# Turned rows go through a scratch in DRAM, and the second norm's rows of blocks 1 to 13 are turned that way

## The chip, the cores and the metric

The kernel runs on one core of a Trainium2 chip. The metric is the device time of one execution in microseconds (us). The core has a TensorE for matmuls (PE), a VectorE (DVE), a ScalarE (ACT), a GpSimd (POOL) and a SyncE (SP), which work through their own instruction queues in order and wait for each other by semaphores. Tiles lie in SBUF or, for results of TensorE, in PSUM. Copies are carried by 16 DMA engines; here practically all copies are issued by SP.

## The reference

A transformer block with adaptive layer norm on `x` of 8 x 1024 x 512 in float32, 16 heads of 32, hidden size 2048:

```python
mod = jax.nn.silu(condition) @ Wada + bada
sh_a, sc_a, gt_a, sh_m, sc_m, gt_m = jnp.split(mod, 6, axis=1)
xn = _layernorm(x, g1, be1)
xm = xn * (1.0 + sc_a[:, None, :]) + sh_a[:, None, :]
x = x + gt_a[:, None, :] * _attention(xm, Wqkv, Wproj, bproj)
xn = _layernorm(x, g2, be2)
xm = xn * (1.0 + sc_m[:, None, :]) + sh_m[:, None, :]
h = jax.nn.gelu(xm @ W1 + b1, approximate=False)
x = x + gt_m[:, None, :] * (h @ W2 + b2)
```

`_attention` is causal multi-head attention with a softmax.

## The kernel before

The rows are cut into 16 blocks of 512 tokens (`blocks`, numbered n; two to a batch entry). For each block there are linear steps: k, q and v projections, the output projection `proj`, the up projection in four parts `u(n,0)` to `u(n,3)`, and the down projection in four parts. The projections use Strassen's scheme: seven products of 256 x 256 tiles in place of eight, from a modulated and transposed input `xm` and three sums and differences of its quarters, `t`. Next to them runs the attention of each block, in score units (`sc`: TensorE writes the scores, VectorE masks them and takes the maxima `mx`) and weight units (`st`: TensorE writes the scores again, ScalarE takes the exponential `pT`, TensorE multiplies with v into `po`). Score units and weight units share one tile of four PSUM banks with a single buffer (`ps_st`), so each such unit waits until the last user of that tile has been read. Three more PSUM banks (`banks`, in the profile `bank`) serve the linear steps.

The order on every engine is written out by a planner that runs when the program is built: it keeps an assumed time for each engine (`now`) and for each tile (`written`, `left`), and always emits the linear thread that would wait least, or attention units where these are behind their pace (`step_aside`, `work`). A thread gives what it needs next by `yield`. The list `plan` sets the order of the linear steps: in window w, with n = w - 1, `proj(n)` is followed by `mt(n)`, which makes the input of the up projection, then by `k` and `q` of block w + 1 and by `u(n,0)`. When the planner finds the linear threads more than 3 us away and all three banks free, it may write a score unit head by head into the banks (`scores_by_heads`).

Weights come through a ring of nine buffers (`wp`, `fetch`): SP issues the load of a piece as soon as the piece nine places earlier has been used. SP's queue is in order, so a copy that waits holds all that stand behind it.

Layer norm (`normalize`) writes normalized rows into the tile `hat` (one buffer), with the tokens in the partitions; the projections need the features there. `modulated(key, ...)` does this turning and applies gain and shift, in one of two ways:

- Keys in `by_pe`: TensorE transposes each 128 x 128 piece into a bank (line 722, 16 transposes a block), and ScalarE or VectorE reads it from there into `xm` (lines 726 and 732).
- Other keys: VectorE transposes within squares of 32 x 32 (line 664, four instructions, into `xm`), and 16 copies of 64 KB from SBUF to SBUF, back into `hat`, move the squares to their places (line 673, function `turn`). ScalarE or VectorE then reads `hat` into `xm`. The order of the tokens differs for these keys; the code in `down` undoes it where it picks columns of `hT`.

Before the change `by_pe` holds every `m` key (the second norm, blocks 0 to 15), and `a0` and `a1`; the `a` keys of blocks 2 to 15 go the second way. `GATHERING` is the time that the planner assumes from the issue of these copies to their end.

## Time and profile before

| what | value |
|---|---|
| median of 3 runs | 3577.96 us (3577.63 to 3582.41) |
| span of the profiled execution, first to last instruction | 3570.9 us |
| TensorE matmuls, mean granted clock | 98% of the span busy, 0.997 |
| VectorE, GpSimd, ScalarE | 61%, 58%, 33% busy |
| bytes moved by DMA | 447 MB, 125 GB/s on the mean |
| copies `hat_a<-xm_a` (line 673) | 224, 64 KB each |

The profiled execution has no separate time; its span stands for it, and the median of the runs is 7.1 us above that span. A row of a group gives line, engine, operation, tiles (written <- read), shapes, count, then busy time in us and the mean duration of one in ns, then the idle time ahead of the group with what ended it. float32 matmuls show as two records each. Busy times of matmuls overlap, so their sum over groups is more than the engine's busy time. A row of the waits gives who waited for whom, then the total in us, the number of waits and the longest. In the timeline the first two figures are the start and the length of a piece in us, and in brackets the idle time before it. A window row gives a stretch, its length, the busy time and count of each engine, the granted TensorE clock, the share of the DMA engines in use and GB/s.

### The profile page before, as it was taken

The numbers are of one execution on the slowest core, as the hardware profiler recorded it, in microseconds if no ns is written. First come the engines' busy times: TensorE is split into PE (matmuls) and PEld (weight loads), VectorE is DVE, ScalarE is ACT, GpSimd is POOL, SyncE is SP. The second block draws the span as 40 slices with busy tenths as digits, with TensorE's granted clock in tenths as the row PEclk, the third lists the DMA queues.
The fourth block names the chain that finished last, engine by engine and source line by source line (L and its number), as shares of the span: only waits on it lengthen the run. The fifth ranks groups of instructions, "written<-read, shape, count | busy, mean of one in ns | idle before, by whom it ended". The sixth has DMA issues, their size and how long they took to land.

```text
span 3570.9 us, 120927 instructions
## 1 busy us (share of the span) xinstructions
PE 3495.3 (98%) x54621; PEld 1749.3 (49%) x54621; DVE 2179.7 (61%) x2393; ACT 1187.1 (33%) x1232; POOL 2080.9 (58%) x2246
## 2 busy tenths in 40 slices
PE   8999899999999999999999999999999999999999
PEld 4444445445554445545454455544545445455445
DVE  5876575564755657465574656746666566565663
ACT  2334333242333513235142342423423134231421
POOL 2667746665466664667545775366762667526660
PEclk9999999999999999999999999999999999999999
DMA  6753433434434344433444334443344433434334
GB/s 200 235 174 93 128 93 110 135 105 138 115 109 131 108 141 113 135 107 105 142 118 146 99 101 141 120 140 102 102 131 124 140 105 104 126 111 140 91 113 137
DMA packets 318934, 447.12 MB, mean 125 GB/s; under 512 B 29516, under 2 KB 179852, under 8 KB 318164
## 3 DMA queue, kind: packets, MB, share of 16 engines
q1 hardware_dynamic: 318304, 439.36, 41.7%
q8 instruction: 430, 7.05, 0.8%
q14 instruction: 84, 0.69, 0.1%
q10 hardware_dynamic: 116, 0.03, 0.0%
HBM read 394.12 MB, written 28.38 MB: 118 GB/s over the span
## 4 chain that ended last, share of the span: by engine, by line
PE 88%; POOL 4%; DMA 3%; DVE 2%; SPq 2%; issue 1%; ACT 1%; ACTq 0%; DVEq 0%; POOLq 0%
PE bank L202 60%; PE sc L1511 8%; PE po L1644 7%; PE st L1604 7%; PE st L1592 2%; POOL pT L1734 2%; PE bank L1665 2%; DMA w<-in_L_cond_Wproj_dram 1%; PE bank L722 1%; SPq L673 1%; POOL hT L161 1%; DVE mx L1528 1%; DMA out_dram<-xr 0%; PE bank L1566 0%; DMA w<-in_L_cond_Wada_dram 0%
## 5 line engine op out<-in xcount | busy, mean ns | idle before, releaser
L1734 POOL TENSOR_TENSOR pT<-pT,pT 128x256 f32<-128x256 f32 (+3 forms) x1254 | 1215.4, 1005 | 335.5 <-PE po L1644 182.2
L1616 ACT ACTIVATE pT<-st 128x2048 f32<-128x2048 f32 x288 | 541.0, 1878 | 1171.6 <-PE st L1604 1074.2
L202 PE MATMUL bank<-w,hT 128*32 128x256 f32 x14336 | 813.0, 380 | 1.1 <-ACT rec L1674 0.9
L1528 DVE TENSOR_REDUCE mx<-sc 128x4 f32<-128x2048 f32 (+3 forms) x384 | 665.8, 1754 | 223.3 <-PE sc L1511 217.1
L202 PEld LDWEIGHTS bank<-w,hT 128*32 128x32 f32 x14336 | 453.0, 110 | 365.7 <-issue 81.0
L202 PE MATMUL bank<-xm_m,w 128*32 128x256 f32 x8192 | 498.2, 380 | 0.0
L202 PE MATMUL bank<-t_m,w 128*32 128x256 f32 x6144 | 383.4, 380 | 0.1
L1621 POOL TENSOR_SCALAR_AFFINE_SELECT pT<-pT 128x512 f32<-128x512 f32 x256 | 168.1, 675 | 344.6 <-ACT pT L1616 344.6
L202 PEld LDWEIGHTS bank<-xm_m,w 128*32 128x32 f32 x8192 | 257.2, 110 | 219.9 <-issue 54.6
L1511 PE MATMUL sc<-kT,qT 32*128 32x512 f32 (+3 forms) x3072 | 329.1, 520 | 2.7 <-DVE mx L1528 1.7
L1525 DVE TENSOR_TENSOR sc<-sc,mask 128x1024 f32<-128x1024 f32 (+1 forms) x160 | 162.7, 1017 | 265.5 <-PE sc L1511 177.5
L1644 PE MATMUL po<-pT,v 128*32 128x512 f32 (+3 forms) x3048 | 303.0, 492 | 2.1 <-POOL pT L1621 2.1
L1604 PE MATMUL st<-qT,kT 32*128 32x512 f32 (+3 forms) x3072 | 301.5, 488 | 0.0
L202 PEld LDWEIGHTS bank<-t_m,w 128*32 128x32 f32 x6144 | 190.2, 110 | 180.8 <-issue 58.1
L202 PE MATMUL bank<-w,qT 128*32 128x512 f32 x2048 | 240.7, 599 | 10.6 <-DMA w<-in_L_cond_Wproj_dram 10.5
L202 PE MATMUL bank<-xm_a,w 128*32 128x256 f32 x3968 | 246.0, 383 | 2.1 <-ACT p_k L188 2.0
L1683 DVE RECIPROCAL rec<-rec 128x128 f32<-128x128 f32 x256 | 224.5, 918 | 33.0 <-ACT rec L1674 33.0
L1511 PEld LDWEIGHTS sc<-kT,qT 32*128 32x128 f32 x3072 | 129.3, 183 | 173.1 <-ACT pT L1616 65.7
L202 PE MATMUL bank<-t_a,w 128*32 128x256 f32 x2944 | 189.6, 382 | 0.4 <-ACT xm_m L732 0.4
L193 DVE TENSOR_TENSOR hT<-bank,u_u 128x512 f32<-128x512 f32 x192 | 129.1, 684 | 98.2 <-PE bank L202 96.9
L1058 ACT ACTIVATE hT<-hT,cols 128x512 f32<-128x512 f32 x256 | 164.4, 711 | 54.6 <-DVE hT L193 54.0
L202 PEld LDWEIGHTS bank<-xm_a,w 128*32 128x32 f32 x3968 | 123.6, 110 | 110.8 <-issue 33.4
(216 smaller groups left out, 3405.6 us busy)
## 6 DMA issues: line engine op xcount, KB each, us to landing
w<-in_L_cond_W_dram SPq DMA_DIRECT2D x384, 256.0 KB
w<-kept_up_S SPq DMA_DIRECT2D x256, 256.0 KB
w<-kept_down_S SPq DMA_DIRECT2D x256, 256.0 KB
w<-kept_qkv_S SPq DMA_DIRECT2D x180, 256.0 KB
w<-in_L_cond_Wqkv_dram SPq DMA_DIRECT2D x147, 256.0 KB
hat_a<-in_x_dram SPq DMA_DIRECT2D x64, 256.0 KB
w<-in_L_cond_Wproj_dram SPq DMA_DIRECT2D x64, 256.0 KB
xr<-in_x_dram SPq DMA_DIRECT2D x64, 256.0 KB
```

What stands on the lines that cost most here:

```text
L193: nc.vector.tensor_tensor(out, src, other, op)
L202: nc.tensor.matmul(ps[r, :], columns, rhs, start=start, stop=stop, skip_group_check=True)
L1058: nc.scalar.activation(hT[:, i, :], hT[:, i, :], AF.Gelu, bias=cols[:, O_B1 + f : O_B1 + f + 1])
L1511: nc.tensor.matmul(sc[:, j, c0 : c0 + w], qTs[n][r, gg, ts(qt, P)], keys_of(n, kh)[r, gg, :w], start=True, stop=True, skip_group_check=True,)
L1525: nc.vector.tensor_tensor(place, place, shape_of.to_broadcast(place.shape), ALU.add)
L1528: nc.vector.tensor_reduce(maxima[n, gg][:, kh, qt, :], sc[:, :, c0 : c0 + w], axis=AX.X, op=ALU.max)
L1604: nc.tensor.matmul(st[:, j, c0 : c0 + w], kT[r, gg, ts(k % NTT, P)], qT[r, gg, TB - w :], start=False, stop=True, skip_group_check=True,)
L1616: nc.scalar.activation(pT[:, :, :used], st[:, :, :used], AF.Exp, scale=scale)
L1621: nc.gpsimd.affine_select(diagonal, diagonal, pattern=[[0, HPG], [1, P]], compare_op=ALU.is_ge, fill=0.0, base=0, channel_multiplier=-1,)
L1644: nc.tensor.matmul(po[r, TB - w :], v[:, k % NTT, g * P + j * hd : g * P + (j + 1) * hd], pT[:, j, c0 : c0 + w], start=(k == 0), stop=last ...
L1683: nc.vector.reciprocal(some, some)
L1734: nc.gpsimd.tensor_tensor(into, into, pT[:, j, c0 : c0 + w], ALU.add)
```

## The change

`by_pe` now holds `a0`, `a1`, `m0`, `m14` and `m15` only, so that the `m` keys of blocks 1 to 13 are turned by VectorE and copies as well. In `turn` the 16 copies from SBUF to SBUF are replaced by one write of the whole tile (1 MB) into a scratch in DRAM, `held`, of which there are two in turn, and four reads of 256 KB from it into `hat`. The planner is told of two waits in place of one: 8 us from the write to the reads, and 8 us from the reads to their use.

```diff
-    by_pe = {f"m{n}" for n in range(NB)} | {"a0", "a1"}
+    by_pe = {"a0", "a1", "m0", f"m{NB - 2}", f"m{NB - 1}"}
...
         for t in range(NTT):
             add_job(lambda t=t: turn_tile(t), [("hat", key, t)], key[0] == "m")
         yield [("blocks", key)], []
+        held = kept.tile([P, NTT * D], F32, tag=f"held_{turns[0] % 2}", name=f"held_{key}")
+        turns[0] += 1
+        nc.sync.dma_start(held, small_blocks)
+        written["held", key] = now["PE"] + HOLDING
+        yield [("held", key)], []
         for m in range(NTT):
-            for a in range(NTT):
-                nc.sync.dma_start(rows[ts(m, Q), a, :], small_blocks[ts(a, Q), ts(m, D)])
-        written["turned", key] = now["PE"] + GATHERING
+            some = held[:, ts(m, D)].rearrange("(a i) d -> i a d", i=Q)
+            nc.sync.dma_start(rows[ts(m, Q), :, :], some)
+        written["turned", key] = now["PE"] + HOLDING
         yield [("turned", key)], []

-    GATHERING = 16000
+    HOLDING = 8000
+    turns = [0]
```

Since the planner places every instruction by these times, the change also moves other instructions on all engines. The built program has 208 transposes fewer on TensorE, 52 square transposes more on VectorE, 135 copies for the turning in place of 224 (27 writes and 108 reads), and 24 matmuls of `scores_by_heads` that were in the ordinary score units before. Lines behind the change are numbered six higher than in the profile of before.

## The prediction

> **What bounds the kernel now.** I read the page first (busy times, then the chain of waits), then the groups of instructions by line and shape, then who waits for whom, and last the timeline and the windows around the places that these named.

> ```profile
> span 3570.9 us, 120927 instructions
> PE 3495.3 (98%) x54621; PEld 1749.3 (49%) x54621; DVE 2179.7 (61%) x2393; ACT 1187.1 (33%) x1232; POOL 2080.9 (58%) x2246
> PE 88%; POOL 4%; DMA 3%; DVE 2%; SPq 2%; issue 1%; ACT 1%; ACTq 0%; DVEq 0%; POOLq 0%
> ```

> TensorE is busy 98% of the span and carries 88% of the chain. It is idle for about 3570.9 - 3495.3 = 76 us in all. So work taken off TensorE shortens the run, and every new idle microsecond on it lengthens the run. What its idle time now consists of:

> ```profile
> PE bank L202 <- DMA w<-kept_qkv_S: 11.7, 7, 2.2
> PE bank L202 <- DMA w<-in_L_cond_Wproj_dram: 10.5, 12, 1.9
> PE bank L202 <- DMA w<-in_L_cond_Wqkv_dram: 3.7, 1, 3.7
> ...
> PE st L1592 <- DVE mx L1528: 8.5, 6, 3.2
> PE sc L1511 <- DVE mx L1528: 1.7, 1, 1.7
> PE sc L1511 <- ACT pT L1616: 1.0, 1, 1.0
> ```

> The first three are waits for weights, 25.9 us; the view cut to 600 to 3060 us gives the same three figures. The last three, 11.2 us, are waits for the one score tile in PSUM (the names `sc` and `st` share one buffer).

> **The change part by part.**

> *1. Transposes taken off TensorE: -32 us.* Blocks 1 to 13 lose 16 transposes each, 208 of the 256 in this row:

> ```profile
> L722 PE MATMUL bank<-ident,hat_m 128*128 128x128 f32 x256 | 43.4, 294 | 4.3 <-ACT hat_m L651 3.3 <-ACT hat_m L624 1.0
> ...
> 1366.30 0.55 PE L722 MATMUL bank<-ident,hat_m 128*128 128x128 f32 x3
> 1366.78 0.64 PE L202 MATMUL bank<-t_a,w 128*32 128x256 f32 x8
> 1367.35 0.77 PE L722 MATMUL bank<-ident,hat_m 128*128 128x128 f32 x5
> 1368.04 1.07 PE L202 MATMUL bank<-t_a,w 128*32 128x256 f32 x16
> 1369.05 1.09 PE L722 MATMUL bank<-ident,hat_m 128*128 128x128 f32 x8
> 1370.07 0.64 PE L202 MATMUL bank<-t_a,w 128*32 128x256 f32 x8
> ```

> By the row they cost at most 43.4 x 208/256 = 35.3 us. From start to start, one block's 16 take 0.48 + 0.69 + 1.02 = 2.19 us, 28.5 us for 13 blocks. I take -32.

> *2. The burst on SP's queue goes: -18 us.* Each of 14 `a` blocks issues 16 small copies in a row:

> ```profile
> 618.93 10.75 SPq L673 DMA_DIRECT2D hat_a<-xm_a  x16
> ...
> L389 SPq DMA_DIRECT2D hat_a<-in_x_dram x56: 315/423/1502, 54.5 to 2916.5; - x56
> ```

> For 10.75 us no weight piece behind them is issued, and the weight waits above follow these bursts. In the change one write and four reads of the second row's shape take their place. At about 0.5 + 4 x 0.42 = 2.2 us of issue, the burst is no longer there. If all of it were caused by the burst, -25.9 us. Against that, the bytes of an `a` turn double to 2 MB, and 13 `m` turns of 2 MB are new: 40 MB, 9% of the 447 MB that are moved now. The reads also hold the queue until the write has landed, with Wproj pieces behind them. So the other end is above nothing: 14 turns at 0.7 us, +10. I take -18, nearer to the end at which the queue is free.

> *3. The new hop itself: hidden, if it takes what a 1 MB move takes here.* No scratch of this size exists before; the nearest row is the one move of 1 MB:

> ```profile
> 425.90 0.53 SPq L981 DMA_DIRECT2D v<-v_early  x1
> 426.40:431.00 4.60, 4.50 (x76) 2.44 (x72) 3.08 (x3) 1.07 (x2) 0.29 (x1) 1.00 0.90 310
> ```

> It is issued at 425.9 and fills the DMA engines (share 0.90) until about 431: 5.1 us. Write and reads: some 10 us, and with other loads between them 8 to 20. What covers them stands in the built order of the changed kernel's instructions: from the last product of `proj(n)` to the first product of `u(n,0)` I add up 37 to 48 us of TensorE work in blocks 2 to 13 (19 or 37 before, mostly). Normalized rows are there early in even blocks:

> ```profile
> 1102.00 1.06 PE L202 MATMUL bank<-w,qT 128*32 128x512 f32 x8
> 1121.00 2.93 ACT L624 ACTIVATE hat_m<-xr,offset_m,rstd_m 128x512 f32<-128x512 f32 x4 [1.91 <-POOL offset_m L608]
> ```

> That is 1121.0 + 2.9 - 1103.1 = 21 us behind the projection; 4 transposes, 10 us of hop and 2 us of modulation bring it to some 36 us. So in even blocks the hop costs nothing. What would wait with it if the cover were gone: behind the modulation on ScalarE the first evacuations of `u(n,0)`, on VectorE the next score reduction, and behind the reads on SP the next pieces of W1, of which nine lie ready by then.

> *4. What fills that wait: +52 us, the term that decides.* The cover is made of k and q of the next block, and when these run out, of attention alone. Then there is nothing to put between two users of the one score tile. The order around `u(5,0)` reads, shortened to its first words:

> ```
> 4107 L202 bank<-t_a7 x15
> 4108 L1517 sc_7_0_0_0 x4
> 4110 L1517 sc_7_0_1_0 x4 [waits DVE]
> 4113 L1598 st_6_3_0 [waits DVE]
> ...
> 4126 L202 bank<-xm_m5 [waits DMA, DVE]
> ```

> Here TensorE must stand until VectorE has reduced one score unit, twice. The trace of before has one such place:

> ```profile
> 439.06 1.14 PE L1511 MATMUL sc<-kT,qT 32*128 32x512 f32 x8 [1.00 <-ACT pT L1616]
> 443.40 0.61 PE L1592 MATMUL st<-mrow,minus_ones 32*128 32x512 bf16 x4 [3.20 <-DVE mx L1528]
> ...
> 440.32 0.70 DVE L1525 TENSOR_TENSOR sc<-sc,mask 128x512 f32<-128x512 f32 x1 [2.84 <-issue]
> 441.05 2.29 DVE L1528 TENSOR_REDUCE mx<-sc 128x4 f32<-128x2048 f32 x1
> ```

> Scores end at 440.20, mask and reduction end at 443.34, and the next user starts at 443.40. I went through both orders and summed, for each pair of neighbours on that tile, how much the TensorE work between them falls short of what the other engine needs:

> ```profile
> L1528 DVE TENSOR_REDUCE mx<-sc 128x4 f32<-128x2048 f32 x192 | 439.8, 2290 | 220.0 <-PE sc L1511 217.1
> L1616 ACT ACTIVATE pT<-st 128x2048 f32<-128x2048 f32 x288 | 541.0, 1878 | 1171.6 <-PE st L1604 1074.2
> ```

> (2.29 us for a reduction of 2048 columns, less for narrower ones, a mask where there is one, 1.88 us for an exponential, 0.2 to 0.3 us of handing over.) Before: 15 us; after: 76 us, nearly all of the difference right ahead of `u(n,0)`, most at blocks 1, 3, 5 and 11. Of the 15 the waits show 11.2, a factor of 0.74. So +45 to +61; I take +52. These waits stay even where the rows are there early, since TensorE keeps its order.

> *5. Six score units go head by head through the three banks* (24 matmuls of `scores_by_heads`, none before). The fourth head waits for a bank that VectorE empties, behind a 2.29 us reduction: up to 2 us each, 0 to 12; I take +6.

> *6. VectorE gets 52 transposes more.*

> ```profile
> L664 DVE STREAM_TRANSPOSE xm_a<-hat_a 128x512 f32<-128x512 f32 x56 | 34.6, 671 | 0.0
> ```

> That is 52 x 0.671 = 35 us on an engine that is idle 39% of the time, so most is hidden. In five blocks two of them stand directly ahead of the first reduction of the stretch in (4): 5 x 1.34 = 7 us if the cover is gone. 0 to 7; I take +4.

> *7. The clock: +13 us.* After a standstill TensorE runs at half rate for a while (columns: stretch, length, busy, clock, DMA share, GB/s):

> ```profile
> 388.00:390.70 2.70, 0.03 (x4) 1.00 0.00 0
> 391.10:394.40 3.30, 3.30 (x20) 0.50 0.00 0
> ...
> 855.70:857.90 2.20, 0.02 (x3) 1.00 0.79 249
> 858.70:862.00 3.30, 3.30 (x40) 0.50 1.06 339
> 113.20:116.20 3.00, 0.02 (x2) 1.00 1.05 384
> 116.20:122.00 5.80, 5.76 (x136) 1.00 1.01 345
> 3052.30:3056.00 3.70, 0.04 (x4) 1.00 0.64 179
> 3056.90:3060.20 3.30, 3.30 (x29) 0.50 1.03 375
> ```

> Three of these four waits bring 3.3 us at 0.50, that is some 1.7 us of lost work. The list in (4) has 11 waits of 2.3 us or more, in seven blocks: 11 x 3/4 x 1.7 = 14, one or two drops of before fall away with (2), and a double wait may bring two stretches: 0 to 28; I take +13. [...]

> *Sum:* -32 - 18 + 0 + 52 + 6 + 4 + 13 = +25 us. Against the profiled execution: span 3570.9 + 25 = 3596. The median of the runs, 3577.96, lies 7.1 us above that span (what is outside first and last instruction), so I forecast 3603 us. For this kernel 0.2%, 7 us, is about what can be told from no change.

> **The rivals.**

> *The saving wins (faster).* Place: the stretch ahead of `u(n,0)`; price: all that it costs, (4) to (7), 75/13 = 5.8 us a block by my sum. It decides from (32 + 18)/13 = 3.8 us a block down. For it speaks that the count overrates (0.74 above) and that the whole 25.9 us of weight waits follow the bursts. Against it, that the waits are fixed in the order. With -35.3 - 25.9 + 45 and nothing else: -16, 3562 us.

> *They cancel (same).* A seam of about 3.8 us: 3578 us.

> *The clock stays up (slower, but less).* If the waits of 2.3 to 2.6 us leave the clock at full rate, as the one at 113.2 did, term (7) is nothing and the time 3590 us. Against it speak the three others in that fence. [...]

> *The turned rows come late (slower still).* In blocks 1, 3 and 11 the reads stand directly behind the write, and the last transposes directly behind the last q product. There the cover is some 10 us of attention and 8 us of its own waits, against 13 us of hop and modulation. For it speaks that weights in flight share the engines (share 1.06 at 858.7); against it, 310 GB/s at 426. If write and reads take 10 us each, `u(n,0)` starts 7 us late in five blocks, with as many more clock drops: 35 + 14, in all +74, 3652 us.

> **How the numbers follow.** My forecast 0.46, the clock stays up 0.10, the saving wins 0.20, they cancel 0.12, late rows 0.12. Slower: 0.46 + 0.10 + 0.12 = 0.68; same 0.12; faster 0.20. The likeliest's own range is 3585 to 3632. To leave out no more than 2 in 10 the range goes from 3562 (the faster case's own value) to 3645 (just short of the late rows').

> **What would show it.** The `L722` row falls from 256 to 48 and its busy time to some 8 us (1). The weight waits on `kept_qkv` and Wproj fall under 10 us (2). TensorE's waits for `mx` and `pT` grow from 11 to about 60 us, placed right ahead of the first products on `xm_m` (4), with a granted clock of 0.50 behind several of them (7). No TensorE wait of more than 1 us on the rows read back (3). Wrong: if the waits for `mx` stay under 30 us, or if the span falls although they grow, (2) was worth more than all weight waits together.

## The result, and the profile after

The changed kernel takes 3627.14 us (median of 4 runs, 3622.46 to 3636.23) against 3577.8 us of the kernel before on the same chip: ratio 1.0147, 95% interval 1.0135 to 1.016, some 52 us slower by the ratio (the medians differ by 49.3 us). The profiled spans differ by 3620.6 - 3570.9 = 49.7 us. The page of the changed kernel (span, busy times, chain of waits by engine):

```profile
span 3620.6 us, 120483 instructions
PE 3488.6 (96%) x54413; PEld 1735.5 (48%) x54413; DVE 2193.8 (61%) x2448; ACT 1197.2 (33%) x1251; POOL 2079.0 (57%) x2240
PE 85%; DVE 6%; DMA 4%; POOL 2%; ACT 1%; issue 1%; SPq 1%; ACTq 0%; DVEq 0%; POOLq 0%
```

TensorE is idle for 3620.6 - 3488.6 = 132 us, 56 more than before, and its busy time falls by 7 us only, although the transposes went as said (groups of instructions, row of the second norm's transposes; it was 43.4 us):

```profile
L728 PE MATMUL bank<-ident,hat_m 128*128 128x128 f32 x48 | 8.3, 310 | 3.4 <-ACT hat_m L651 3.4
```

So 35 us of work left and some 29 us of slower work took its place. The recorded clock says the same: between 100 us and the last microseconds, 0.50 is granted in six stretches before, 24 us in all, and in 16 stretches after, 82 us; half of the 58 us between them is 29 us of lost work. The idle time, from the view of who waits for whom (us in total, number of waits, longest):

```profile
PE st L1598 <- DVE mx L1534: 34.2, 26, 3.8
PE sc L1517 <- DVE mx L1534: 15.1, 9, 3.1
PE bank L1485 <- DVE mx L1504: 10.2, 6, 2.2
PE bank L202 <- ACT v L188: 9.7, 3, 5.2
PE po L1650 <- POOL pT L1627: 7.1, 2, 5.5
...
PE bank L202 <- DMA w<-in_L_cond_Wproj_dram: 6.9, 5, 2.9
...
PE sc L1517 <- ACT pT L1622: 5.9, 5, 2.6
...
PE st L1598 <- ACT pT L1622: 3.1, 4, 1.1
...
PE bank L202 <- ACT p_v L188: 2.2, 2, 1.5
...
PE bank L202 <- DVE u_v L193: 2.1, 1, 2.1
```

Waits for the score tile (the two rows of `mx` on line 1534 and the two of `pT` on line 1622) go from 11.2 to 58.3 us, and those of the scores taken head by head (line 1485) are 10.2 us where there was nothing: +57. Weight waits go from 25.9 to 6.9 us: -19. New are 14 us behind `v`, `p_v` and `u_v`, and 5 us behind GpSimd at the end. With the row of transposes and the clock: -35 + 29 + 57 - 19 + 14 + 5 = +51, against 49.7 measured.

The waits behind `v` are turned rows that come late. ScalarE and VectorE wait for the rows of the first norm that were read back (the same view, of ScalarE and of VectorE):

```profile
ACT xm_a L738 <- DMA hat_a<-held_a: 74.5, 12, 11.8
...
DVE xm_a L732 <- DMA hat_a<-held_a: 44.1, 9, 8.7
```

Before, the same two rows were 7.6 and 1.5 us. The turned rows of the second norm are waited for too, but less: 12.8 us by ScalarE and 14.6 us by VectorE, 5.7 us at the longest, and TensorE's own waits for `xm_m` are 1.8 us. One place where rows of the first norm come late, in the timeline (start, duration, engine, in brackets the idle time ahead):

```profile
1948.65 0.38 SPq L673 DMA_DIRECT2D held_a<-xm_a  x1
...
1961.18 1.31 SPq L1104 DMA_DIRECT2D out_dram<-xr  x2
...
1963.08 1.81 SPq L678 DMA_DIRECT2D hat_a<-held_a  x4
...
1971.55 2.22 ACT L738 ACTIVATE xm_a<-hat_a,shifta,gaina 128x512 f32<-128x512 f32 x3 [6.92 <-DMA hat_a<-held_a]
1973.68 0.56 ACT L188 COPY v<-bank 128x512 f32<-128x512 f32 x1
...
1974.30 3.55 PE L202 MATMUL bank<-w,t_a 128*32 128x256 f32 x32 [5.18 <-ACT v L188]
```

The four reads are issued 14 us after the write, behind an output store in SP's queue; the rows can be used 8.5 us later; an evacuation of `v` (the copy of a result out of its bank) that needs none of them stands behind the modulation in ScalarE's queue, and TensorE waits for that one. No row of TensorE's own waits names the late rows.

The last thing to see is how far the two kernels are apart along the run, by the end of the last product of `proj(n)` in each trace: after block 1 the changed kernel is 10.7 us ahead, after block 7 it is 15.4 us behind, after block 14 34.4 us, after block 15 49.2 us. So nearly 15 us of the 50 are lost in the last block, in which nothing is turned differently.

### The profile page after: what moved, and what is told of

It is laid out like the page before. It is cut to its first block, busy times and chain, and to the rows that moved or that the text cites. A ratio compares the mean times of both kernels' runs of the same rounds, so it can differ in the third digit from the quotient of the medians.

```text
span 3620.6 us, 120483 instructions
## 1 busy us (share of the span) xinstructions
PE 3488.6 (96%) x54413; PEld 1735.5 (48%) x54413; DVE 2193.8 (61%) x2448; ACT 1197.2 (33%) x1251; POOL 2079.0 (57%) x2240
## 4 chain that ended last, share of the span: by engine, by line
PE 85%; DVE 6%; DMA 4%; POOL 2%; ACT 1%; issue 1%; SPq 1%; ACTq 0%; DVEq 0%; POOLq 0%
PE bank L202 59%; PE sc L1517 8%; PE po L1650 6%; PE st L1610 6%; DVE mx L1534 3%; PE st L1598 2%; PE bank L1671 2%; DMA hat_a<-held_a 1%; POOL pT L1740 1%; DMA hat_m<-held_m 1%; DMA w<-in_L_cond_Wproj_dram 1%; DVE sc L1531 1%; ACT pT L1622 1%; SPq L678 0%; ACT xm_a L738 0%
## 5 line engine op out<-in xcount | busy, mean ns | idle before, releaser
L1622 ACT ACTIVATE pT<-st 128x2048 f32<-128x2048 f32 x288 | 541.0, 1879 | 1097.2 <-PE st L1610 987.9
L202 PE MATMUL bank<-w,hT 128*32 128x256 f32 x14336 | 818.0, 380 | 0.0
L1534 DVE TENSOR_REDUCE mx<-sc 128x4 f32<-128x2048 f32 (+3 forms) x378 | 652.1, 1746 | 217.1 <-PE sc L1517 211.2
L202 PEld LDWEIGHTS bank<-w,hT 128*32 128x32 f32 x14336 | 447.1, 110 | 381.7 <-issue 98.1
L202 PE MATMUL bank<-xm_m,w 128*32 128x256 f32 x8192 | 497.7, 384 | 1.8 <-DVE xm_m L732 1.0
L202 PE MATMUL bank<-t_m,w 128*32 128x256 f32 x6144 | 378.5, 380 | 0.9 <-DVE t_m L748 0.8
L202 PEld LDWEIGHTS bank<-xm_m,w 128*32 128x32 f32 x8192 | 256.6, 111 | 227.8 <-issue 51.9
L1517 PE MATMUL sc<-kT,qT 32*128 32x512 f32 (+3 forms) x3024 | 328.3, 521 | 21.4 <-DVE mx L1534 15.1
L202 PEld LDWEIGHTS bank<-t_m,w 128*32 128x32 f32 x6144 | 191.5, 110 | 163.5 <-issue 34.8
L1689 DVE RECIPROCAL rec<-rec 128x128 f32<-128x128 f32 x256 | 225.7, 920 | 54.5 <-ACT rec L1680 54.5
L202 PE MATMUL bank<-w,qT 128*32 128x512 f32 x2048 | 243.4, 606 | 7.0 <-DMA w<-in_L_cond_Wproj_dram 6.9
L202 PE MATMUL bank<-xm_a,w 128*32 128x256 f32 x3968 | 244.2, 382 | 0.2 <-DVE u_q L193 0.2
L1517 PEld LDWEIGHTS sc<-kT,qT 32*128 32x128 f32 x3024 | 129.7, 184 | 211.3 <-issue 86.7
L1714 POOL TENSOR_TENSOR qT<-top,rec 128x512 f32<-128x512 f32 x61 | 82.1, 1345 | 198.2 <-DVE rec L1689 177.6
L202 PE MATMUL bank<-t_a,w 128*32 128x256 f32 x2944 | 183.7, 380 | 0.0
L202 PEld LDWEIGHTS bank<-xm_a,w 128*32 128x32 f32 x3968 | 124.5, 110 | 109.0 <-issue 32.3
```

Source lines behind the costliest of these rows:

```text
L202: nc.tensor.matmul(ps[r, :], columns, rhs, start=start, stop=stop, skip_group_check=True)
L1517: nc.tensor.matmul(sc[:, j, c0 : c0 + w], qTs[n][r, gg, ts(qt, P)], keys_of(n, kh)[r, gg, :w], start=True, stop=True, skip_group_check=True,)
L1534: nc.vector.tensor_reduce(maxima[n, gg][:, kh, qt, :], sc[:, :, c0 : c0 + w], axis=AX.X, op=ALU.max)
L1622: nc.scalar.activation(pT[:, :, :used], st[:, :, :used], AF.Exp, scale=scale)
L1689: nc.vector.reciprocal(some, some)
L1714: nc.gpsimd.tensor_tensor(qTs[n][:, g, :], top, rec, ALU.mult)
```

## The experiments

The ratio after each is that to the kernel before, run on the same chip between the runs of the experiment, with its 95% interval; "us" beside a ratio is (ratio - 1) x 3575.

**The two halves of the change.** `a_scratch` keeps the second norm on TensorE, `m_scratch` keeps the 16 copies for the `a` rows.

```diff
# a_scratch, to the changed kernel
-    by_pe = {"a0", "a1", "m0", f"m{NB - 2}", f"m{NB - 1}"}
+    by_pe = {f"m{n}" for n in range(NB)} | {"a0", "a1"}
# m_scratch, in turn()
+        if key[0] == "a":
+            for m in range(NTT):
+                for a in range(NTT):
+                    nc.sync.dma_start(rows[ts(m, Q), a, :], small_blocks[ts(a, Q), ts(m, D)])
+            written["turned", key] = now["PE"] + GATHERING
+            yield [("turned", key)], []
+            return
```

> The change for the `a` rows alone: every second norm stays on TensorE as before, the 14 `a` turns go by one write and four reads. TensorE's built order is nearly that of before, so there are no new seams. Theory 1 (what the trace after suggests): the weight waits fall by about 19 us, but the turned `a` rows come late through SP's queue, and TensorE stands 5 to 15 us behind the evacuations that wait with them on ScalarE and VectorE; net -15 to 0, 3563 to 3578 us. Rival (term 2 of the forecast in full, nothing comes late): -18 or better, 3550 to 3561 us, and no TensorE wait on v's evacuations.

> The change for the `m` rows alone: blocks 1 to 13 through the scratch, the `a` rows by their 16 copies as before. Theory 1 (seams and the clock are the loss): transposes -32, waits for the score tile +57, clock +25, weight waits stay at some 25 us: +45 to +65, 3623 to 3643 us. Rival (the late `a` rows and the end of the kernel are most of what the forecast missed): without them +25 or less, 3595 to 3605 us.

`a_scratch`: 3561.04 us, 0.9968 (0.9958 to 0.9978), -11 us. Of the three rows of weight waits that the prediction names (25.9 us) one is left:

```profile
PE bank L202 <- DMA w<-in_L_cond_Wproj_dram: 17.4, 14, 2.4
```

`m_scratch`: 3632.93 us, 1.016 (1.0145 to 1.0175), +57 us. The loss is the `m` half's; the late `a` rows are not most of it. The halves add up to +46, near the whole.

**The hop taken out, or its cover shortened.** `no_hop` turns the `m` rows on VectorE as in the change but neither writes nor reads them, so that its second norm's product is computed on unturned rows; `hold5` plans 5 us for each half of a hop instead of 8.

```diff
# no_hop, in turn(), ahead of the write
+        if key[0] == "m":
+            written["turned", key] = written["blocks", key]
+            return
# hold5
-    HOLDING = 8000
+    HOLDING = 5000
```

> The changed kernel without the hop of the `m` rows: VectorE turns the 52 tiles as in the change, but nothing is written to or read from the scratch for them, and the modulation reads the rows unturned (the second norm's product is so computed on wrong rows; the `a` turns are as changed). Theory 1 (the cover that is planned for the hop makes the seams, and the hop is the whole price): the count of shortfalls is 24 us against 76, transposes -35, seams +7, clock +3, `a` rows -12: 3535 to 3548 us. Rival (VectorE's 52 transposes and their place in its queue cost it): 3560 us or more.

> The changed kernel with the planned time of each half of the hop 5 us, not 8, so that u(n,0) is planned some 6 us earlier; by the count of the order the shortfalls on the score tile go from 76 to 46 us, and 4 score matmuls go head by head, not 24. Theory 1 (the seams come from the plan's own allowance): waits for the score tile about -22, clock -5 to -10: 3592 to 3605 us, and waits on the rows read back under 5 us. Rival (the hop really needs the 16 us): TensorE waits for the rows of the second norm instead, 13 times 2 us or more, and the time stays at 3615 to 3640 us.

`no_hop`: 3552.94 us, 0.9947 (0.9935 to 0.9959), -19 us. The 13 hops therefore cost 52 + 19 = 71 us in the change, 5.5 us each. But without any hop the transposes gain 19 - 11 = 8 us over `a_scratch`, not the 25 that theory 1 gave. `hold5`: 3688.21 us, 1.0319 (1.0306 to 1.0333), +114 us, worse than the rival. TensorE's waits in `hold5`, in the view of who waits for whom:

```profile
PE st L1598 <- DVE mx L1534: 23.2, 17, 3.8
...
PE bank L202 <- ACT p_v L188: 14.2, 2, 7.4
PE bank L202 <- ACT mrow L1578: 13.6, 2, 9.3
PE bank L202 <- ACT xm_m L738: 13.2, 4, 6.1
PE bank L202 <- ACT v L188: 13.0, 2, 6.9
```

The waits for `mx` fall by 11 us with the shorter seams (a seam is the run of waits for the score tile ahead of `u(n,0)`), and several times as much comes back behind ScalarE's queue. ScalarE's own waits for the rows read back into `hat_m` grow from 12.8 us in the change to 44.2 us. In the trace of the changed kernel the 13 hops take 12 to 20 us from the issue of the write to the first modulation, so 10 us cannot be enough.

**Idle products in the waits.** If the clock is half of the loss, work without use in the waits should win some of it back.

```diff
+    def fill(reads):
+        wait = wait_of((reads, ["st"]))
+        idle = [i for i in range(3) if not live[i] and left.get(("l", i), 0.0) <= now["PE"]]
+        if wait < 1500 or not idle:
+            return
+        for _ in range(int((wait - 400) // 170)):  # fill2: (wait - 700) // 250
+            nc.tensor.matmul(banks[idle[0]][:, :P], ident, ident, start=True, stop=True, skip_group_check=True)
...
         step_aside(reads, ["st"])
+        fill(reads)
```

> The changed kernel, in which 212 idle products of ident on ident (128 columns, a free bank, some 0.17 us each, 36 us in all) stand in 16 of the planned waits for the score tile, each run shorter than its wait. Theory 1 (half of what the seams cost is TensorE's halved clock after them): the stretches at a granted 0.50 fall from 82 us to under 45 us and the time by 12 to 25 us, 3602 to 3615 us, though work was added. Rival (the clock is no part of it): the fillers change nothing or delay, 3625 to 3650 us.

> The `fill` kernel with shorter runs of idle products: in `fill` one took 0.25 us, not 0.17, so that the runs overran their waits by some 13 us. Now each run is sized at 0.25 us and ends 0.7 us before its planned wait. Theory 1 (the halved clock after the seams is worth some 25 us): no overrun is left, the stretches at 0.50 stay at or under the 58 us of `fill`, and the time falls to 3606 to 3618 us. Rival (the clock costs little): 3623 to 3632 us.

`fill`: 3628.46 us, 1.0153 (1.014 to 1.0166), as slow as the change. The idle products are 48.5 us in its trace, the waits for the score tile fall by some 35 us only, and the stretches at 0.50 fall from 82 to 58 us: what the clock gave, the overrun took. `fill2`: 3616.51 us, 1.0124 (1.0108 to 1.0141), 8 us under the change, stretches 51 us. This goes theory 1's way, at the weak end; `mended` below shows it again and more clearly.

**The reads on another queue, and even blocks alone.**

```diff
# after_act
-            nc.sync.dma_start(rows[ts(m, Q), :, :], some)
+            nc.scalar.dma_start(rows[ts(m, Q), :, :], some)
# as_even
-    by_pe = {"a0", "a1", "m0", f"m{NB - 2}", f"m{NB - 1}"}
+    by_pe = {"a0", "a1", "m0", f"m{NB - 2}", f"m{NB - 1}"} | {f"m{n}" for n in range(1, NB, 2)}
```

> The changed kernel with the four reads of each turn issued from ScalarE's queue, the write still on SP's; the built order on TensorE is the same. Theory 1 (the `a` rows are late because their reads stand behind SP's stores and weight pieces): from write to first read falls from 8 to 14 us in most `a` turns to about 5, TensorE's waits behind v's and u_v's evacuations (14 us) go, 3608 to 3618 us. Rival (the rows are late because the two moves of 1 MB take that long on the engines of the DMA): the gap stays, 3622 to 3632 us; and if ScalarE, whose queue now waits for the write to land, holds up exponentials, 3632 us or more.

> The changed kernel with the second norm turned through the scratch in blocks 2, 4, 6, 8, 10 and 12 alone, where the normalized rows are ready early; the odd blocks' rows stay on TensorE. 96 transposes go (-16 us); the count of shortfalls is 30 us, against 15 before and 76 in the change. Theory 1 (a block costs what its seam costs, and here the seams are few): -16 + 11 + clock 4 - 12 for the `a` rows: 3555 to 3568 us, no worse than `a_scratch` (3561). Rival (every `m` turn costs its hop wherever it stands, 57/13 = 4.4 us net a block): 6 x 4.4 = 26 above `a_scratch`, 3580 to 3592 us.

`after_act`: 3641.64 us, 1.0196 (1.0181 to 1.021), 17 us worse than the change. On ScalarE's queue the reads wait for the write in front of exponentials and evacuations: in its trace `pT` waits 9.1 + 8.5 us and `v` 13.0 us for rows read back, which they don't use. Moving the reads there cures nothing. `as_even`: 3586.7 us, 1.0047 (1.0033 to 1.0061), +17 us, 28 above `a_scratch`; the rival. That is 28/6 = 4.7 us net a block, where `m_scratch` has 57/13 = 4.4: by this count a hop in an even block, where the normalized rows are early, costs as much as one elsewhere. Late `a` rows are in the 28 us too, though: TensorE's waits behind `v` and `p_v` are 15.0 us in this trace, 6.6 us in `a_scratch`.

**The plan's own times.** The planner counts 16 transposes on TensorE for each block's second norm, turned or not, and steers the pace of linear work by that sum. `rate_m` leaves out those that are not made; `rate_late` plans the `a` hops at 2 x 11 us besides; `a_scr_late` is `a_scratch` with 2 x 11 us; `mended` is `rate_late` with the idle products of `fill2`.

```diff
# rate_m
-        return parts + sum(costs.get(step[0], 0) for step in plan[w])
+        skipped = [step for step in plan[w] if step[0] in ('mt',) and f"{step[0][0]}{step[1]}" not in by_pe]
+        return parts + sum(costs.get(step[0], 0) for step in plan[w] if step not in skipped)
# rate_late and a_scr_late, twice in turn()
-        written["held", key] = now["PE"] + HOLDING
+        written["held", key] = now["PE"] + (HOLDING if key[0] == "m" else 11000)
```

> The changed kernel, whose plan no longer counts 16 transposes on TensorE for the second norm of a block that is turned elsewhere (the planned time of a stretch counts them in the change too, so linear work runs ahead of attention by 1.7 us a block, 22 us at the end). In the built order 172 more entries of products on hT stand behind the last score tile than in the change, as many as before. Theory 1 (the change loses some 15 us behind block 14, because no linear work is left to cover the last block's exponentials and POOL's work on them): TensorE's wait for POOL's pT falls from 7.1 to some 2 us, the 10.2 us at 0.50 behind it go, 3611 to 3616 us. Rival (the loss at the end has another cause): the last block keeps its 230 us, 3622 to 3632 us.

> `rate_m` with the planned time of each half of an `a` hop at 11 us, not 8 (the `m` hops stay at 8); the count of shortfalls is the same, 81 us. Theory 1 (the `a` rows come 3 to 6 us later than planned, and what is planned behind them makes TensorE wait): the waits behind v, u_v and p_v fall from 14 to under 5 us and the time by 6 to 14 us against `rate_m`. Rival (the rows are late by chance of the queue and a longer plan only moves the stalls): within 4 us of `rate_m`.

> `a_scratch` (the scratch for the `a` rows alone) with the planned time of each half of the hop at 11 us. Theory 1: the 7.5 us of waits behind v fall under 3 us, 3552 to 3558 us, the fastest kernel so far. Rival: 3559 to 3566 us.

> `rate_late` with the sized idle products of `fill2` in the planned waits for the score tile. Theory 1 (what is left of the loss is the seams and half of the clock's loss): 8 to 14 us below `rate_late`, but still not under `a_scratch`, since the seams themselves (55 us of waits, filled or not) outweigh the 35 us of transposes: 3580 to 3598 us. Rival (the clock and the late rows were the whole loss, seams cost little): below 3565 us.

`rate_m`: 3648.19 us, 1.0204 (1.0188 to 1.022), 20 us slower than the change, against both expectations. Yet the step that it was made for came as expected. From the end of `proj(14)` to that of `proj(15)` it takes 215.5 us, before 215.0, in the change 229.8. The timeline of that place in the changed kernel (start, duration, engine, and in brackets the idle time ahead):

```profile
3477.37 4.50 PE L202 MATMUL bank<-w,hT 128*32 128x256 f32 x80
3482.88 0.40 PE L1598 MATMUL st<-mrow,minus_ones 32*128 32x384 bf16 x8 [1.01 <-ACT pT L1622]
3483.10 1.10 PE L1610 MATMUL st<-qT,kT 32*128 32x384 f32 x16
3484.13 1.06 PE L1650 MATMUL po<-pT,v 128*32 128x512 f32 x8
3490.70 1.94 PE L1650 MATMUL po<-pT,v 128*32 128x384 f32 x16 [5.50 <-POOL pT L1627]
```

The same place in the timeline of the kernel before:

```profile
3424.41 3.66 PE L202 MATMUL bank<-w,hT 128*32 128x256 f32 x64
3430.12 1.06 PE L1644 MATMUL po<-pT,v 128*32 128x512 f32 x8 [2.05 <-POOL pT L1621]
3431.00 3.64 PE L202 MATMUL bank<-w,hT 128*32 128x256 f32 x64
3434.46 1.05 PE L1644 MATMUL po<-pT,v 128*32 128x384 f32 x16
```

And in the timeline of `rate_m`:

```profile
3489.82 3.66 PE L202 MATMUL bank<-w,hT 128*32 128x256 f32 x64
3495.52 1.59 PE L1651 MATMUL po<-pT,v 128*32 128x512 f32 x8 [2.04 <-POOL pT L1628]
3496.87 4.86 PE L202 MATMUL bank<-w,hT 128*32 128x256 f32 x64
```

Before, products on `hT` stand between the last uses of the exponentials; in the change they have been used up, and TensorE waits 5.5 us for GpSimd, then runs 10.2 us at 0.50. In `rate_m` they are there again. That is the cause of the 15 us in the last block. What `rate_m` loses, it loses before that: at the end of `proj(14)` it is 65.4 us behind the kernel before, the change 34.4. Its waits for Wproj are 21.2 us (6.9 in the change) and those of the scores taken head by head 21.6 us (10.2); ScalarE and VectorE wait 66.2 and 47.6 us for `hat_a`, about as long as in the change. So the end can be mended, but no run shows that this alone makes the change faster.

`rate_late`: 3588.85 us, 1.0049 (1.0034 to 1.0064): 55 us under `rate_m`, four times theory 1's most. `a_scr_late`: 3536.89 us, 0.9899 (0.9884 to 0.9914), -36 us and 25 under `a_scratch`; the fastest kernel here that computes the whole block, faster than both that were given. TensorE's waits in its trace (ScalarE's and VectorE's for `hat_a` are 1.1 and 6.0 us, in `a_scratch` 69.3 and 50.9):

```profile
PE st L1598 <- DVE mx L1534: 11.6, 13, 1.6
...
PE bank L202 <- DMA w<-in_L_cond_Wproj_dram: 0.7, 1, 0.7
```

There is hardly a weight wait left, and none behind `v`. So theory 1 holds in its direction, with the size wrong by a factor: `a` rows that were planned at 16 us and took 15 to 23 (19 on the mean, in the trace of the change) cost far more than the 7 us of TensorE waits behind `v` and `p_v` in `a_scratch`. Not all of it is traced to a wait: from `rate_m` to `rate_late` TensorE's idle time falls by 36 us and its busy time by 18 us, and the stretches at 0.50 (92 and 89 us) don't explain the second. `mended`: 3578.86 us, 1.0018 (1.0009 to 1.0027), 11 us under `rate_late`; the stretches at 0.50 fall from 89 to 38 us. Work without use, 11 us gained: the clock's loss is real.

**What is left to tell apart.** `before_g22` is the kernel before with its copies planned at 22 us; `no_hop_rl`, `even_late` and `m11` are `rate_late` without the `m` hops, with `m` turns in even blocks alone, and with 2 x 11 us for the `m` hops too.

```diff
# before_g22
-    GATHERING = 16000
+    GATHERING = 22000
# no_hop_rl: rate_late with the lines of no_hop; even_late: with the line of as_even, and the `a` transposes left out of the planned time too
# m11
-    HOLDING = 8000
+    HOLDING = 11000
```

> The kernel before (16 copies for an `a` turn, every second norm on TensorE), with the planned time of the copies at 22 us, as in `a_scr_late`, not 16. Theory 1 (the `a` path was planned too early in every kernel so far, and the later time is the gain, not the scratch): 3537 to 3552 us, waits for weights mostly gone. Rival (the 16 copies in a row on SP's queue were the cost and the scratch's five issues are the gain): 3565 to 3580 us, with some 25 us of weight waits as before.

> `rate_late` without the hop of the `m` rows (turned on VectorE, not written or read back; the second norm's product is computed on unturned rows). Theory 1: with the `a` rows on time only the saved transposes are left: `a_scr_late` (3537) - 35 + 3: 3500 to 3512 us, and the 13 hops cost `rate_late` (3589) minus this, some 80 us, 6 us each. Rival (VectorE's transposes or the shorter cover cost a good part): 3520 us or more.

> `as_even` (only the blocks 2, 4, 6, 8, 10 and 12 turn their `m` rows through the scratch) with the corrected planned time and 11 us for each half of an `a` hop. The count of shortfalls is 26 us against 18 in `a_scr_late`. Theory 1 (what as_even lost against a_scratch was mostly the late `a` rows): 3537 - 16 + 6 + clock 4: 3526 to 3538 us. Rival (an `m` hop costs its 4 to 5 us net wherever it stands): 3552 to 3565 us.

> `rate_late` with 11 us for each half of an `m` hop too, so that both kinds of rows are planned at 22 us. The count of shortfalls goes from 81 to 101 us, and 72 score matmuls go head by head, not 36. Theory 1 (the `m` rows are on time at 16 us, a longer plan only lengthens the seams): 12 to 25 us above `rate_late`, 3600 to 3614 us. Rival (the `m` rows come late as the `a` rows did, and stall ScalarE and VectorE): 3565 to 3582 us.

`before_g22`: 3561.29 us, 0.9965 (0.9952 to 0.9979), -13 us, between the two ranges. Its weight waits, in the same view:

```profile
PE bank L202 <- DMA w<-kept_qkv_S: 9.6, 8, 2.0
...
PE bank L202 <- DMA w<-in_L_cond_Wqkv_dram: 4.9, 3, 3.2
...
PE bank L202 <- DMA w<-in_L_cond_Wproj_dram: 2.6, 1, 2.6
```

17 us with 16 copies, 0.7 us in `a_scr_late` with five: the later plan alone is worth 13 us, the scratch alone 11, both together 36. With the same planned time on both sides the scratch is worth 23 us. `no_hop_rl`: 3525.95 us, 0.9869 (0.9855 to 0.9882), -47 us, but only 11 under `a_scr_late`: the rival. Against `rate_late` the 13 hops cost 17 + 47 = 64 us, 4.9 each. `even_late`: 3555.53 us, 0.9948 (0.9936 to 0.9961), 18 above `a_scr_late`: again the rival's range. But it differs from `a_scr_late` in a second thing, the `a` transposes left out of the planned time, and `a_rate_late` below shows that this alone costs 9 us. Against `a_rate_late` it is 8 us, 1.4 net a block, with 11 us more of waits for `mx`. So a hop in an even block isn't free, but whether it costs as much as one elsewhere stays open. `m11`: 3637.9 us, 1.0178 (1.0164 to 1.0192), 46 above `rate_late`: theory 1's direction, at twice its size. The stretches at 0.50 grow from 89 to 133 us. So the `m` rows are near enough on time at 16 us (3.5 and 3.9 us of waits for `hat_m` on ScalarE and VectorE in `rate_late`), and each way from there is worse: `hold5` against the change, `m11` against `rate_late`.

**Why do 208 transposes give 11 us?**

```diff
# extra_turns, to a_scr_late, behind TensorE's transpose of tile t
+                    if c == 0 and key[0] == "m" and 0 < int(key[1:]) < NB - 2:
...
+                        nc.vector.transpose(into, got[:, t, :].rearrange("p (h m i) -> p h m i", m=NTT, i=Q))
+                        note("DVE", 620, [("hat", key, t)], [("unused", key, t)])
# a_rate_late: a_scr_late, planned time without the 14 turned `a` blocks' transposes
```

> `a_scr_late` (second norm on TensorE, 208 transposes kept) with 52 transposes more on VectorE: in blocks 1 to 13 each normalized tile is also turned into the buffer that the modulation then overwrites, so that VectorE does what it does in the change and nothing else is moved. TensorE's built order is the same. 52 x 0.671 = 35 us of work on VectorE. Theory 1 (TensorE's transposes stood where it would have waited for VectorE anyway, so taking them off gives waits for mx back): +2 to +9 us, 3539 to 3546 us. Rival (VectorE's transposes delay the reductions behind them and so TensorE): +15 to +25 us, 3552 to 3562 us.

> `a_scr_late` with the 14 `a` turns' transposes taken out of the planned time. The built order changes little (shortfalls 15 us against 18). Theory 1 (in this order the run-ahead of linear work is harmless, the end has its cover): 3532 to 3541 us. Rival (run-ahead costs as it did in the change): 3520 to 3530 us.

`extra_turns`: 3556.18 us, 0.9949 (0.9934 to 0.9963), 18 above `a_scr_late`, the rival's range. The trace does not bear the rival out, though: TensorE's waits for `mx` are 14.8 us, in `a_scr_late` 14.9. The longest row of who waits for whom is another:

```profile
PE bank L728 <- ACT xm_m L744: 11.8, 5, 4.6
```

Of the 18 us, 11.8 are waits of TensorE's own transposes for a bank, which the modulation empties late because it now writes where VectorE has just written (ScalarE's modulation waits 13.2 us for VectorE's write, in `a_scr_late` it has no such wait): an order that the change doesn't have. The stretches at 0.50 grow from 10 to 31 us besides. Up to block 7 the kernel is 3 us behind. So neither theory is shown by its time. What the pair `no_hop_rl` and `a_scr_late` shows is where the gain went. The row of transposes falls by 38 us (47.3 to 9.2). The wait of the weight units for `mx`, 11.6 us in the fence of `a_scr_late` above, is in the trace of `no_hop_rl`:

```profile
PE st L1602 <- DVE mx L1538: 25.2, 23, 2.5
```

All idle time of TensorE rises by 20 us, and the stretches at 0.50 go from 10 to 27 us (8 us of work): -38 + 20 + 8 = -10. `a_rate_late`: 3547.5 us, 0.9925 (0.9912 to 0.9939), 9 slower than `a_scr_late`, outside both ranges. In its trace ScalarE waits for the rows read back again, where `a_scr_late` has 1.1 us:

```profile
ACT xm_a L739 <- DMA hat_a<-held_a: 65.1, 9, 8.7
```

TensorE's waits for GpSimd's `pT` are 9.3 us (2.0 in `a_scr_late`). What brings this about was not found. It is no rule that a truer planned time is faster.

## Why the prediction was right and wrong

The direction was right and so were the signs of the terms that could be measured, and the time lay in the range, but the move was twice the forecast: +52 instead of +25 us. Step by step:

1. *Transposes off TensorE, -32.* The row fell by 35 us as said. Counted as a saving it was too good: with no hop at all they gave 8 us (`no_hop`) or 11 (`no_hop_rl`). A part is the last block, 14.4 us in `no_hop` alone: the plan still counted the transposes, so linear work ran ahead and was missing at the end (shown by `rate_m`). The order of the instructions had this to be read; the forecast looked only ahead of `u(n,0)`. The rest came back as waits for `mx` and clock.
2. *The burst gone, -18.* Weight waits fell by 19, as forecast, but the burst is not all of it. In `a_scratch`, where only the burst goes, they fall by 8.5 us, from 25.9 to 17.4: the 15.4 us on `kept_qkv` and Wqkv vanish, and those on Wproj grow from 10.5 to 17.4 us. In `m_scratch`, which keeps the burst, they fall too, to 18.7 us. So the size was in part luck; alone the `a` half brought 11 us. The 0.7 us a turn at the term's upper end stands in no row.
3. *The hop hidden, 0.* For the `m` rows a hop of 8 to 20 us was forecast and 12 to 20 measured, and `u(n,0)` began within 2 us of the last modulation in 12 of 13 blocks, 4.5 us behind it in the other; TensorE stood for these rows in its own name for 1.8 us only. For the `a` rows it was wrong: nothing was set down for them, and they cost 14 us of waits behind `v`, `p_v` and `u_v`, with clock on top. "No TensorE wait of more than 1 us on the rows read back" was nearly true and looked in the wrong place: the waits bear the name of the evacuations queued behind.
4. *(4) and (5): waits for the score tile, 52 + 6.* 47 + 10 = 57 measured. The count through the built order, times 0.74, held. "In even blocks the hop costs nothing" did not: `as_even` lost 4.7 us net for each of its six, late `a` rows included, and `even_late` 1.4 us for each against `a_rate_late`. Which is nearer is open.
5. *(6) VectorE, +4.* Not settled. `extra_turns` shows no longer waits for `mx` from the 52 transposes, but it stalls on an order that the change doesn't have.
6. *(7) The clock, +13.* 29 measured. Stretches at 0.50 did come behind such waits (82 us of them in all, 24 before), but the size was wrong: 11 waits times three quarters times one stretch of 3.4 us, where the seams bring 3.4 to 13.7 us each, and the late `a` rows (3.4 us behind the wait for `v` at 1974, for one) and the end (10.2 us) more.

The failed steps are thus (7), sized at less than half (16 us), (3) for the `a` rows (14 us), and the end of the kernel, which no step had (5 us of waits, and its clock in (7)); against them stand 3 us more in (1), 1 in (2) and 5 less in (4) to (6), all from the trace after. By experiment the same miss reads: hops 71 us against 75 in terms (4) to (7), `a` rows -11 against -18, and transposes -8 against -32. This count puts the clock and the end of the kernel that took the transposes' place under the transposes, and the late `a` rows under the `a` rows.

Of the rivals, "the clock stays up" is out, and "the turned rows come late" came true for the rows that it did not mean. "The saving wins" could not hold: even with the `a` rows planned later and the end mended (`rate_late`), 13 hops cost 64 us against the 11 that the transposes bring.

## What to carry to other kernels

Work taken off the engine that sets the time is worth its length only where something else is ready in its place (here the row of transposes fell by 38 us from `a_scr_late` to `no_hop_rl`, the time by 11): read in the built order what now covers each wait, up to the last block, and whether a planner still counts what is gone. When a data path changes, measure its new latency and give that to the planner: 11 us for each half in place of 8 was worth 25 us here, on a path that no wait of TensorE named; but time each such step, since a truer plan can also be slower (`rate_m`, `a_rate_late`). Turning rows by a DRAM scratch pays where there is time between the turning and the use (`a_scr_late`, 1% under the kernel before), not where attention alone has to fill it (`rate_late`, where the 13 hops cost 64 us).

## What the runs showed of the hardware

One seam of the change (stretch, length, busy, clock, DMA share, GB/s):

```profile
482.60:486.00 3.40, 0.81 (x8) 1.00 0.80 321
486.00:489.40 3.40, 1.01 (x12) 0.50 0.47 120
489.40:492.80 3.40, 3.40 (x24) 0.50 1.03 213
492.80:496.20 3.40, 2.58 (x22) 1.00 0.07 14
```

Two waits, 3.1 and 2.4 us, fall into neighbouring steps (0.81 and 1.01 us of 3.4 busy), and two steps run at 0.50, from 486.0 to 492.8. Three steps of the kernel before, around the wait of 3.0 us in the prediction that was followed by no 0.50, and around one of 2.2 us that was:

```profile
111.20:114.60 3.40, 2.02 (x108) 1.00 1.01 341
114.60:118.00 3.40, 1.76 (x72) 1.00 1.05 377
...
855.30:858.70 3.40, 1.21 (x24) 1.00 0.79 248
```

The wait at 113.2 lies across two steps and leaves each busy by more than half (2.02 and 1.76 of 3.4 us); the shorter one at 855.7 lies in one (1.21 us busy), and the stretch at 0.50 begins at its end, 858.7.
